# An attention block on one core: where a head's projection products stand among its scores and weighted sums

## The chip, the cores and the metric

The kernel runs on one core of a Trainium2 chip. A core has five engines, each with its own queue of instructions that it works through in order: TensorE (PE, matmuls; its weight loads are listed apart as PEld), VectorE (DVE), ScalarE (ACT), GpSimd (POOL) and SyncE (SP, which only issues transfers here). The metric is the time of one execution on the device in microseconds (us); lower is better.

## The reference

For each of 16 images of 512 channels and 32 x 32 pixels: a group normalisation, q, k and v by one 1x1 convolution, attention with 4 heads of 128 channels over the 1024 pixels, an output projection, and the input added.

```python
xn = ((xg - mu) * jax.lax.rsqrt(var + EPS)).reshape(b, c, h, w)
qkv = jnp.einsum('oc,bchw->bohw', qkv_w, xn) + qkv_b[:, None, None]
...
attn = jax.nn.softmax(jnp.einsum('bhnd,bhmd->bhnm', q, k) * scale, axis=-1)
out = jnp.einsum('bhnm,bhmd->bhnd', attn, v)
...
out = jnp.einsum('oc,bchw->bohw', proj_w, out) + proj_b[:, None, None]
return x + out
```

## The kernel before

Everything is float32. The attention runs over 16 images (b) x 4 heads (h) x 8 key blocks (j) of 128 keys, 512 steps in all. Each step has two halves of 512 queries. A half issues one matmul of scores into a PSUM bank (`s`, line 862), an exponential by ScalarE into `p` (868), and one matmul of the weighted sum of the step before (`po`, 935): the sum lags the scores by one step, so its input has long been there. VectorE adds the finished `p` of a step to a running total (`tot`, 881). A float32 matmul is two passes in the profile, so it appears as two records.

Between these matmuls stand the projections of other data. Each head carries one of them: head 0 the q and k of this image's heads 2 and 3 (`qk_1`), head 1 the output projection of the image before (`pp`), head 2 the q and k of the next image's heads 0 and 1 (`qk_0`), head 3 the next image's v. Each is a matrix product computed by a two-level Strassen scheme. The outer level has seven products, taken in four groups (`OUTER`): three groups of two and, as the last (group 3), a single one. Inside a group the inner level has again seven products, in the order 1, 2, 6, 5, 7, 4, 3 (`strassen`, whose units are the entries of a plan), so that one projection is 28 units. A unit of a group of two is two matmuls of 256 columns (four records), of group 3 one.

Two PSUM banks serve a group. Products 1, 6, 7 and 4 accumulate one after the other in bank `x`: after 1, 6 and 7 ScalarE copies the bank out (`p1`, `u2`, `u3`, line 502), and the next product waits for that copy. Product 2 has a bank `y` of its own; products 5 and 3 share another. VectorE adds a bank and a copy into a result (line 646): c11 from product 2 and `p1`; c22 from product 5's bank and `u3`; c12 from the same bank and `u2`, once product 3 is added to it. So product 3 waits until VectorE has read the bank for c22. c21 is copied by ScalarE (644). For v, VectorE then adds groups (695, 784) and transposes in blocks of 32 (787), and GpSimd sends the result to DRAM (795) and back in another layout (800).

A tile framework orders the instructions of each engine from dependencies, priorities and the order in which the code traces them; it may put a matmul ahead of one traced before it. `tc.issue_after(ins)` makes all instructions of the same engine that its block traces stand behind `ins` in that engine's queue; it adds no wait and doesn't touch other engines.

Before the change `plan_head` spreads the 28 units over 8 key blocks (7 for v) with `spread`. The loop at the end of `fast_path` runs a key block's units after the scores and the weighted sum of each half, the first half of the list behind the first half's sum, the rest behind the second's:

```python
if s > 0:
    weighted_sum(s - 1, half)
n = (len(units) + 1) // 2
run(units[half * n : (half + 1) * n])
```

In the text, "j5.1" is key block 5, second half, and "g3:4" is product 4 of group 3.

Of the kernel before, what the change touches and what calls it, by code (L numbers as in the profile page):

```python
# [186 lines left out]
def fast_path(ctx, tc, x, sources, out, consts, flag, dims):  # L187
# [6 lines left out]
    nc = tc.nc  # L194
    B, C, N, NCC, NH2, NB, GC, SCALE = dims
# [288 lines left out]
    def run(units):  # L484
        for u in units:
            u()
# [322 lines left out]
    def v_block(b, h, j):  # L809
        v, n = vs[b, h // 2], NB // NH2  # L810
        return v[:, h % 2, j, :] if b == 0 else v[:, j // n, h % 2, :, j % n]

    def proj_groups(b):

        ys = {}

        def place(which, r):
            return 2 * (int(which[1]) - 1) + r, int(which[2]) - 1

        def prepare(which, r):  # L820
            o, half = place(which, r)

            own = which == "c12"
            t = ys[which, r] = (tpool if own else ypool).tile(
                [P, HALF], F32, tag=f"ot4{r}" if own else "y", name=f"y_{b}_{o}_{half}"
            )

            eng = nc.sync if own else nc.gpsimd
            dma = eng.dma_start(t, x[b, ts(o, P), ts(half, HALF)])

            tc.add_manual_dep(
                dma.ins, last_eviction[b].ins.name,
                mybir.DependencyInfo(
                    mybir.DependencyClass.Sync, mybir.DependencyReason.DATA
                ),
                reason="residual",
            )

        def finish(which, r, a, c):
            o, half = place(which, r)  # L840
            t = ys.pop((which, r))
            nc.vector.scalar_tensor_tensor(
                t, a, projb_sb[:, o : o + 1], t, ALU.add, ALU.add
            )
            nc.vector.tensor_add(t, t, c)
            nc.gpsimd.dma_start(out[b, ts(o, P), ts(half, HALF)], t)  # L846

        return two_levels(f"pp_{b}", "proj", b, lambda: ob[b], finish, prepare=prepare)
# [4 lines left out]
    steps = B * HEADS * NB  # L853

    def where(s):
        bh, j = divmod(s, NB)
        return (*divmod(bh, HEADS), j)
# [72 lines left out]
    def weighted_sum(s, half):  # L930
        b, h, j = where(s)
        if j == 0:
            po[half] = ps_o.tile([P, HALF], F32, tag=f"o{half}", name=f"po_{b}_{h}_{half}")
        i = ts(half, HALF)
        nc.tensor.matmul(  # L935
            po[half], v_block(b, h, j), ps[s][:, i],
            start=(j == 0), stop=(j == NB - 1),
        )
        if j == NB - 1:
            if (b, h) not in os_:  # L940
                os_[b, h] = opool.tile([P, N], F32, tag="o", name=f"o_{b}_{h}")
            last_eviction[b] = nc.scalar.copy(os_[b, h][:, i], po[half])

    def divide(b, h):
        nc.vector.tensor_mul(os_[b, h], os_[b, h], rinv.pop((b, h)))

    def spread(plan, units, first, last):

        for i, u in enumerate(units):
            plan[first + i * (last - first) // len(units)].append(u)  # L950

    def bias_of_v(o):

        acc = ps_a.tile([P, HALF], F32, tag="y", name=f"pb_{o}")
        half, r = divmod(o, 2)
        for c in range(NCC):
            block = stage["proj"][f"a{half + 1}{c // KC + 1}"]
            nc.tensor.matmul(
                acc[:, 0:1], block[:, ts(r * KC + c % KC, P)], vb_sb[:, c : c + 1],
                start=(c == 0), stop=(c == NCC - 1),  # L960
            )
        nc.vector.tensor_add(
            projb_sb[:, o : o + 1], projb_sb[:, o : o + 1], acc[:, 0:1]
        )

    def kept_group(site, g):
        if g == 0:
            stage_sums(site)
        group_weights(site, g, True)

    def staggered(lists, starts=None):


        starts = starts or (0, 4, 8, 16)[: len(lists)]
        at = [(a + i, g, u) for g, (a, us) in enumerate(zip(starts, lists))
              for i, u in enumerate(us)]
        return [u for _, _, u in sorted(at, key=lambda t: t[:2])]
# [104 lines left out]
    def plan_head(b, h):  # L1082

        plan = [[] for _ in range(NB)]
        if h == 0:
            spread(plan, staggered(next_qk.pop()), 0, NB)
            if b > 0:
                plan[6].append(lambda: o_blocks(b - 1))
                plan[6].append(lambda: sums_of_b(ob[b - 1]))
            else:  # L1090
                plan[5].append(lambda: stage_blocks("v"))
        elif h == 1:
            if b > 0:
                spread(plan, staggered(proj_groups(b - 1)), 0, NB)
            if b + 1 == B:
                plan[0].append(lambda: last_loads("x"))
            else:
                plan[0].append(lambda: load_x(b + 1))
                spread(plan, [lambda c=c: stats_chunk(b + 1, c) for c in range(NCC)], 2, 4)
                gather, scale = stats_group(b + 1)  # L1100
                if b == 0:
                    plan[4] += [gather, scale]
                else:
                    plan[4].insert(0, gather)
                    plan[5].insert(0, scale)
                for r in range(2):
                    plan[5 + r] += [

                        lambda c=c, half=half: normalise(b + 1, c, half, b > 0 or c % 2 == 1)
                        for c in range(KC * r, KC * r + KC) for half in range(NH2)  # L1110
                    ]
                plan[6].append(lambda: x_sums(b + 1, (1,)))
            if b == 0:
                for g in range(len(OUTER)):
                    plan[g // 2].append(lambda g=g: kept_group("v", g))
                    plan[NB // 2 - 1 + g].append(lambda g=g: kept_group("proj", g))
                plan[2].append(lambda: stage_blocks("proj"))
                spread(plan, [lambda o=o: bias_of_v(o) for o in range(NCC)], 3, 5)
        elif b + 1 == B:
            if h == 2:  # L1120
                plan[0].append(lambda: last_loads("w"))
                plan[2].append(last_bias)
            else:
                os_[b, h] = opool.tile([P, N], F32, tag="o", name=f"o_{b}_{h}")
                plan[3].append(lambda: o_blocks(b))
                plan[3].append(lambda: sums_of_b(ob[b], (1,)))
                plan[5].append(lambda: sums_of_b(ob[b], (2, 3), (0,)))
        elif h == 2:
            spread(plan, staggered(qk_groups(b + 1, 0)), 0, NB)

            plan[0].insert(2, lambda: x_sums(b + 1, (2,)))
            plan[1].append(lambda: x_sums(b + 1, (3,)))
        else:

            spread(plan, staggered(next_v.pop()), 0, NB - 1)

            plan[NB - 2].append(lambda: ahead[f"qk_{b + 1}_1"]())
        return plan
# [87 lines left out]
    next_v, next_qk = [], [qk_groups(0, 1)]  # L1226
# [4 lines left out]
    plan = []  # L1231
    for s in range(steps + 1):
        units = []
        if s < steps:
            b, h, j = where(s)
            if j == 0:
                plan = plan_head(b, h)
            units = plan[j]
            if j == NB - 1 and h == 2 and b + 1 < B:
                next_v.append(v_groups(b + 1))  # L1240
                next_qk.append(qk_groups(b + 1, 1))
                units.append(ahead[f"v_{b + 1}"])
        if NB < s < steps and s % NB == 1:
            denominators(*where(s - 2)[:2])
        for half in range(NH2):
            if s < steps:
                scores(s, half)
                if j in (1, 2) and half == 1 and s > NB:
                    with tc.issue_after(exps[s].ins):
                        spread_inverse(*where(s - NB)[:2], j - 1)  # L1250
                if half == 1 and j == 4 and s > NB:

                    with tc.issue_after(added[b, h, 4].ins):
                        divide(*where(s - NB)[:2])
            if s > 0:
                weighted_sum(s - 1, half)
            n = (len(units) + 1) // 2
            run(units[half * n : (half + 1) * n])
        if s < steps and h == 1 and j == 6 and 0 < b < B - 1:
            running_sum(s, 1)  # L1260
        if s > 0:
            del ps[s - 1]
# [136 lines left out]
```

## Time and profile before

| | us |
|---|---|
| three runs | 3161.3, 3164.14, 3161.74 |
| median | 3161.74 |
| profiled execution | 3160.22 |
| its span, first to last instruction | 3158.5 |
| time of one late image (826.64 to 1021.85) | 195.21 |
| VectorE busy in that image | 165.18 |
| ScalarE busy in that image | 90.48 |

How to read the profile's lines: a group's line gives the source line, the engine, the operation, the tiles (output<-inputs), their shapes and the count, then the busy time and the mean duration of one record in ns, then the engine's idle time before them and what ended it. A timeline line gives the start, the time that the merged instructions cover, engine, line, operation, tiles, shapes and count, and in brackets the idle time before and what ended it. Consecutive records of one group are merged (x2, x4). Records of matmuls overlap because matmuls are pipelined, so the time that a matmul costs is read from start to start.

### The profile page before, as it was taken

The numbers are of one execution on the slowest core, as the hardware profiler recorded it, in microseconds if no ns is written. First come the engines' busy times: TensorE is split into PE (matmuls) and PEld (weight loads), VectorE is DVE, ScalarE is ACT, GpSimd is POOL, SyncE is SP. The second block draws the span as 40 slices with busy tenths as digits, with TensorE's granted clock in tenths as the row PEclk, the third lists the DMA queues.
The fourth block names the chain that finished last, engine by engine and source line by source line (L and its number), as shares of the span: only waits on it lengthen the run. The fifth ranks groups of instructions, "written<-read, shape, count | busy, mean of one in ns | idle before, by whom it ended". The sixth has DMA issues, their size and how long they took to land.

```text
span 3158.5 us, 34075 instructions
## 1 busy us (share of the span) xinstructions
PE 3147.1 (100%) x10442; PEld 2181.1 (69%) x10442; DVE 2655.5 (84%) x4687; ACT 1433.7 (45%) x2651; POOL 497.0 (16%) x897
## 2 busy tenths in 40 slices
PE   9999999999999999999999999999999999999999
PEld 7566676676766767677767677677676676767764
DVE  9878979788897888978889787997879978799785
ACT  3535435354353543535435454353534535344433
POOL 0011121111211112111121111212012120121200
PEclk9999999999999999999999999999999999999999
DMA  5555554546545455554555545555455554555531
GB/s 176 187 185 159 184 178 149 177 146 200 167 160 165 150 195 174 167 162 147 193 170 169 169 146 192 168 170 173 142 182 172 174 176 138 179 166 177 188 123 48
DMA packets 210668, 524.83 MB, mean 166 GB/s; under 512 B 32176, under 2 KB 65456, under 8 KB 210480
## 3 DMA queue, kind: packets, MB, share of 16 engines
q1 hardware_dynamic: 133088, 282.39, 28.9%
q0 software_dynamic: 64000, 204.54, 19.2%
q10 hardware_dynamic: 13392, 35.66, 3.5%
q8 instruction: 86, 1.41, 0.2%
q14 instruction: 102, 0.84, 0.1%
HBM read 389.30 MB, written 133.17 MB: 165 GB/s over the span
## 4 chain that ended last, share of the span: by engine, by line
PE 96%; DVE 2%; DMA 1%; issue 0%; SPq 0%; ACT 0%; POOL 0%; ACTq 0%; DVEq 0%; POOLq 0%
PE po L935 27%; PE s L862 27%; PE qk_x L622 12%; PE qk_y L622 9%; PE pp_x L622 6%; PE v_x L622 6%; PE v_y L622 4%; PE pp_y L622 4%; PE lx L1022 0%; DVE qk_t L590 0%; DMA x<-in_x 0%; PE ly L1022 0%; SPq L373 0%; DVE qk L730 0%; DVE qk_r L646 0%
## 5 line engine op out<-in xcount | busy, mean ns | idle before, releaser
L935 PE MATMUL po<-p,v 128*128 128x512 f32 x2048 | 1047.8, 593 | 0.7 <-ACT p L868 0.7
L862 PE MATMUL s<-qk,qk 128*128 128x512 f32 x2048 | 1046.3, 592 | 0.3 <-DVE qk L730 0.3
L868 ACT ACTIVATE p<-s 128x512 f32<-128x512 f32 x1024 | 610.4, 596 | 947.4 <-PE s L862 909.9
L935 PEld LDWEIGHTS po<-p,v 128*128 128x128 f32 x2048 | 604.4, 302 | 320.5 <-issue 213.3
L881 DVE TENSOR_TENSOR tot<-tot,p 128x1024 f32<-128x1024 f32 x385 | 469.5, 1219 | 166.1 <-ACT p L868 166.1
L862 PEld LDWEIGHTS s<-qk,qk 128*128 128x128 f32 x2048 | 388.7, 190 | 89.8 <-issue 29.2
L622 PEld LDWEIGHTS qk_x<-qk_t,w 128*128 128x128 f32 x1344 | 251.7, 190 | 166.7 <-issue 75.3
L622 PE MATMUL qk_x<-qk_t,w 128*128 128x256 f32 x1344 | 356.6, 382 | 0.1
L502 ACT COPY qk_u<-qk_x 128x512 f32<-128x512 f32 (+1 forms) x256 | 136.2, 532 | 230.1 <-PE qk_x L622 230.1
L795 POOL DMA_DIRECT2D vd<-vu x120 | 66.7, 557 | 894.9 <-DVE vu L787 891.7
L646 DVE TENSOR_TENSOR qk_r<-qk_y,qk_u 128x512 f32<-128x512 f32 (+1 forms) x256 | 157.7, 616 | 34.9 <-ACT qk_u L502 21.6
L596 POOL DMA_DIRECT2D kept_t<-qk_t x240 | 129.3, 540 | 274.5 <-DVE qk_t L590 203.9
L646 DVE TENSOR_TENSOR v_r<-v_y,v_u 128x512 f32<-128x512 f32 (+1 forms) x120 | 76.2, 635 | 110.6 <-ACT v_u L502 80.3
L622 PEld LDWEIGHTS pp_x<-pp_t,w_proj 128*128 128x128 f32 x630 | 116.0, 190 | 76.9 <-issue 25.6
L622 PE MATMUL pp_x<-pp_t,w_proj 128*128 128x256 f32 x630 | 168.8, 385 | 0.0
L800 POOL DMA_DIRECT2D v<-vd x240 | 140.6, 592 | 168.1 <-DMA vd<-vu 68.3
L622 PE MATMUL v_x<-v_t,w_v 128*128 128x256 f32 x630 | 166.6, 381 | 0.0
L846 POOL DMA_DIRECT2D out_y<-y x120 | 65.1, 543 | 603.9 <-DVE groups L293 400.6
L622 PEld LDWEIGHTS v_x<-v_t,w_v 128*128 128x128 f32 x630 | 118.4, 190 | 55.3 <-issue 19.1
L622 PE MATMUL qk_y<-x,w 128*128 128x256 f32 x512 | 142.1, 379 | 0.0
L730 DVE SCALAR_TENSOR_TENSOR qk<-qk_r,qkb_sb,qk_r 128x512 f32<-128x512 f32 x192 | 137.6, 743 | 1.6
L502 ACT COPY v_u<-v_x 128x512 f32<-128x512 f32 (+1 forms) x124 | 66.2, 534 | 157.2 <-PE v_x L622 130.4
(214 smaller groups left out, 4449.8 us busy)
## 6 DMA issues: line engine op xcount, KB each, us to landing
w<-kept SPq DMA_DIRECT2D x90, 512.0 KB, 3.9
kept_t<-qk_t POOLq DMA_DIRECT2D x180, 256.0 KB, 3.2
v_t<-kept_t SPq DMA_DIRECT2D x180, 256.0 KB, 2.9
w<-kept SPq DMA_DIRECT2D x90, 384.0 KB, 3.7
rinv<-row ACTq DMA_DIRECT2D x63, 512.0 KB, 4.8
x<-in_x POOLq DMA_DIRECT2D x60, 512.0 KB, 5.0
vd<-vu POOLq DMA_DIRECT2D x120, 256.0 KB, 3.1
v<-vd POOLq DMA_DIRECT2D x240, 128.0 KB, 4.0
```

The costliest lines, as they stand in the source:

```text
L502: nc.scalar.copy(t[n][:, :width], t["x"][:, :width])
L596: nc.gpsimd.dma_start(t, to)
L622: nc.tensor.matmul(acc[:, ts(i, Q)], have["w"][t][:, i, slot, :], inner(i, bn), start=(first and i == 0), stop=True, skip_group_check=True,)
L646: nc.vector.tensor_add(dst, view(a), view(c))
L730: nc.vector.scalar_tensor_tensor(st[b, h][:, ts(half, HALF)], a, qkb_sb[:, i : i + 1], c, ALU.add, ALU.add)
L795: nc.gpsimd.dma_start(rows[which][ts(h, P), :], u)
L800: nc.gpsimd.dma_start(vs[b, pair][ts(q, BLK), half].rearrange("m h (k i) j -> m (h k) (i j)", k=n), rows[which].rearrange("(k m) (q e) -> ...
L846: nc.gpsimd.dma_start(out[b, ts(o, P), ts(half, HALF)], t)
L862: nc.tensor.matmul(sc, ks[b, h][:, ts(j, P)], qs[b, h][:, ts(half, HALF)], start=True, stop=True)
L868: exps[s] = nc.scalar.activation(ps[s][:, ts(half, HALF)], sc, AF.Exp, scale=SCALE)
L881: added[b, h, j] = nc.vector.tensor_add(tot[b, h][:, i], tot[b, h][:, i], ps[s][:, i])
L935: nc.tensor.matmul(po[half], v_block(b, h, j), ps[s][:, i], start=(j == 0), stop=(j == NB - 1),)
```

## The change

The plan of a head keeps empty places where its products stood, and the products go into a list `halfway` by halves: `SIZES` says how many each half takes, 16 halves for a projection laid out over 8 key blocks and 15 for v. In the loop each half takes the next entry of `halfway` and traces it inside `issue_after` of that half's weighted sum, before the half's other units. Other units of the plan run where their index puts them, as before.

```diff
-        nc.tensor.matmul(
+        summed = nc.tensor.matmul(
             po[half], v_block(b, h, j), ps[s][:, i],
             start=(j == 0), stop=(j == NB - 1),
         )
...
+        return summed
...
+    SIZES = {NB: (2, 2, 2, 1, 2, 2, 2, 1, 2, 2, 1, 2, 2, 2, 1, 2),
+             NB - 1: (2, 2, 2, 2, 2, 2, 2, 2, 2, 1, 2, 2, 2, 1, 2)}
+    halfway = []
+
+    def products(plan, units, last):
+        spread(plan, [None] * len(units), 0, last)
+        assert sum(SIZES[last]) == len(units)
+        for n in SIZES[last]:
+            halfway.append(units[:n])
+            units = units[n:]
...
         plan = [[] for _ in range(NB)]
+        halfway.clear()
         if h == 0:
-            spread(plan, staggered(next_qk.pop()), 0, NB)
+            products(plan, staggered(next_qk.pop()), NB)
...
-                spread(plan, staggered(proj_groups(b - 1)), 0, NB)
+                products(plan, staggered(proj_groups(b - 1)), NB)
...
-            spread(plan, staggered(qk_groups(b + 1, 0)), 0, NB)
+            products(plan, staggered(qk_groups(b + 1, 0)), NB)
...
-            spread(plan, staggered(next_v.pop()), 0, NB - 1)
+            products(plan, staggered(next_v.pop()), NB - 1)
...
+            behind = nullcontext()
             if s > 0:
-                weighted_sum(s - 1, half)
+                behind = tc.issue_after(weighted_sum(s - 1, half).ins)
+            if halfway and s < steps:
+                with behind:
+                    run(halfway.pop(0))
             n = (len(units) + 1) // 2
-            run(units[half * n : (half + 1) * n])
+            run(u for u in units[half * n : (half + 1) * n] if u)
```

## The prediction

> **What bounds the kernel now.** I read the page first, then the groups by line with shapes kept apart, then the timeline of one late image (its first scores at 826.64 us, the next image's at 1021.85 us), engine by engine. The page's busy line, clock line and chain of waits:
>
> ```profile
> PE 3147.1 (100%) x10442; PEld 2181.1 (69%) x10442; DVE 2655.5 (84%) x4687; ACT 1433.7 (45%) x2651; POOL 497.0 (16%) x897
> PEclk9999999999999999999999999999999999999999
> PE 96%; DVE 2%; DMA 1%; issue 0%; SPq 0%; ACT 0%; POOL 0%; ACTq 0%; DVEq 0%; POOLq 0%
> ```
>
> TensorE is never shown idle and its clock is full, so no other engine's speed matters by itself. What is left is hidden inside the matmuls' own durations: a matmul held up by its weights is drawn longer, not later. The groups show how much of that there is (count, then busy us and mean ns of one):
>
> ```profile
> L935 PE MATMUL po<-p,v 128*128 128x512 f32 x2048 | 1047.8, 593 | 0.7 <-ACT p L868 0.7
> L862 PE MATMUL s<-qk,qk 128*128 128x512 f32 x2048 | 1046.3, 592 | 0.3 <-DVE qk L730 0.3
> L622 PE MATMUL qk_x<-qk_t,w 128*128 128x256 f32 x1344 | 356.6, 382 | 0.1
> L622 PE MATMUL pp_x<-pp_t,w_proj 128*128 128x256 f32 x630 | 168.8, 385 | 0.0
> L622 PE MATMUL v_x<-v_t,w_v 128*128 128x256 f32 x630 | 166.6, 381 | 0.0
> L622 PE MATMUL v_y<-x,w_v 128*128 128x256 f32 x240 | 67.9, 385 | 0.0
> L622 PE MATMUL v_y<-v_t,w_v 128*128 128x256 f32 x210 | 55.1, 379 | 0.0
> ```
>
> Taking 379 ns as the unhindered 256-column pass, the three x groups carry 3 x 1344 + 6 x 630 + 2 x 630 = 9.1 us too much, v_y 6 x 240 = 1.4 us, and po, against the scores, 1 x 2048 = 2.0 us. So reordering products can win at most about 12.5 us, 0.4% of the span. The end of head 3 in the late image shows all three kinds, on TensorE:
>
> ```profile
> 1006.61 1.02 PE L862 MATMUL s<-qk,qk 128*128 128x512 f32 x2
> 1007.46 1.11 PE L622 MATMUL v_x<-v_t,w_v 128*128 128x256 f32 x4
> 1008.41 1.04 PE L935 MATMUL po<-p,v 128*128 128x512 f32 x2
> 1009.28 1.03 PE L622 MATMUL v_y<-xt,w_v 128*128 128x256 f32 x4
> ...
> 1015.31 0.59 PE L622 MATMUL v_x<-v_t,w_v 128*128 128x256 f32 x2
> 1015.74 1.02 PE L862 MATMUL s<-qk,qk 128*128 128x512 f32 x2
> 1016.60 0.59 PE L622 MATMUL v_x<-v_t,w_v 128*128 128x256 f32 x2
> 1017.03 1.04 PE L935 MATMUL po<-p,v 128*128 128x512 f32 x2
> 1017.90 0.68 PE L622 MATMUL v_y<-x,w_v 128*128 128x256 f32 x2
> 1018.42 1.02 PE L862 MATMUL s<-qk,qk 128*128 128x512 f32 x2
> ...
> 1021.85 1.02 PE L862 MATMUL s<-qk,qk 128*128 128x512 f32 x2
> ```
>
> One score or weighted sum takes 0.86 us from start to start (1018.42 to 1021.85 holds four), a two-part product 0.86, a single one 0.43.
> First kind: the v_x product at 1007.46 (product 4 of group 2) follows product 7 in the same bank with only scores between; it takes 0.95 instead of 0.86. Its weight load waits for the copy out of the bank:
>
> ```profile
> 1006.80 0.58 ACT L502 COPY v_u<-v_x 128x512 f32<-128x512 f32 x1 [1.12 <-PE v_x L622]
> 1007.44 0.73 PEld L622 LDWEIGHTS v_x<-v_t,w_v 128*128 128x128 f32 x4 [0.65 <-ACT v_u L502]
> ```
>
> Second kind: a weighted sum behind a product instead of behind scores (1.04 against 1.02). Its weight load, by the group of the loads, takes 302 ns, and the last pass of a product that could cover it is 0.22 us (half of 0.43):
>
> ```profile
> L935 PEld LDWEIGHTS po<-p,v 128*128 128x128 f32 x2048 | 604.4, 302 | 320.5 <-issue 213.3 <-ACT pp_u L502 3.3 <-ACT p L868 1.5
> ```
>
> Third kind: v_y at 1017.90 (product 3 of group 3) takes 0.68 instead of 0.59. It accumulates into the y bank that VectorE must have read, and VectorE is what to look at:
>
> ```profile
> 998.83 1.23 DVE L881 TENSOR_TENSOR tot<-tot,p 128x1024 f32<-128x1024 f32 x1 [3.62 <-ACT p L868]
> ...
> 1017.07 0.43 DVE L646 TENSOR_TENSOR v_r<-v_y,v_p 128x256 f32<-128x256 f32 x1
> 1017.40 0.43 DVE L646 TENSOR_TENSOR v_r<-v_y,v_u 128x256 f32<-128x256 f32 x1
> 1017.73 1.09 DVE L787 STREAM_TRANSPOSE vu<-vt 128x512 f32<-128x512 f32 x1
> 1018.66 0.68 DVE L784 TENSOR_TENSOR vt<-v_r 128x512 f32<-128x512 f32 x1
> 1019.26 1.21 DVE L881 TENSOR_TENSOR tot<-tot,p 128x1024 f32<-128x1024 f32 x1
> 1020.38 0.42 DVE L646 TENSOR_TENSOR v_r<-v_y,v_u 128x256 f32<-128x256 f32 x1
> ...
> 1023.33 1.15 DVE L787 STREAM_TRANSPOSE vu<-vt 128x512 f32<-128x512 f32 x1 [0.67 <-DMA vd<-vu]
> ```
>
> The add at 1017.40 is c22 (bank y after product 5, plus copy u3); it ends at 1017.83 and product 3 really starts 0.16 later (1017.90 plus the 0.09). The add at 1020.38 is c12, which product 3 makes possible. From 1000.9 to 1022.6 VectorE works off a backlog, as the busy times of that stretch show (its length, then TensorE, weight loads, VectorE, ScalarE, GpSimd): VectorE is busy in 21.67 of 21.70 us.
>
> ```profile
> 1000.90:1022.60 21.70, 21.70 (x68) 14.42 (x67) 21.67 (x32) 7.91 (x15) 4.57 (x8) 1.00 0.52 167
> ```
>
> **The change part by part.** No instruction is added or dropped; only orders change. In the built programs, on TensorE, every product now stands behind its half's weighted sum, and two stretches are shared out anew: the first products of the output projection, and the end of the v projection (numbers are the seven products of a group, PO the weighted sum, g the group):
>
> ```
> head 3   before                 after
> j5.0     s g2:4 PO g2:3 g3:1    s PO g2:4 g2:3
> j5.1     s PO g3:2 g3:6         s PO g3:1 g3:2
> j6.0     s PO g3:5 g3:7         s PO g3:6 g3:5
> j6.1     s g3:4 PO g3:3         s PO g3:7
> j7.0     s PO                   s PO g3:4 g3:3
> j7.1     s PO                   s PO
> ```
>
> On VectorE only this end of v changes, once per image in the 15 images that prepare a next one: c11, c22, transpose, vt, tot, c12 becomes c11, transpose, vt, tot, c22, transpose, vt, qk_t, c12 (and one vu transpose passes the reciprocal). SyncE's queue is the same. On GpSimd the next residual loads pass behind x loads, and a half's v write moves ahead of four v reads; all are used a head later or more. On ScalarE copies and exponentials swap places with a full 0.86 us of weighted sum between.
>
> Removed copy waits (first kind). They stand in one half each of heads 0, 1, 2 and 3, at the start of the projection and near its end:
>
> ```profile
> 1074.04 1.11 PE L622 MATMUL pp_x<-pp_t,w_proj 128*128 128x256 f32 x4
> ...
> 1113.40 0.67 PE L622 MATMUL pp_x<-pp_t,w_proj 128*128 128x256 f32 x2
> ```
>
> Each is 0.08 by length, 0.09 by spacing (0.95 - 0.86): 0.085 us. Behind the weighted sum the copy gets 0.86 us more cover (0.43 in the last of these places), so all go: six an image. One of the six, in head 1, gains nothing, because its product 3 already starts on VectorE's heels:
>
> ```profile
> 1107.82 0.68 DVE L646 TENSOR_TENSOR pp_r<-pp_y,pp_u 128x512 f32<-128x512 f32 x1
> 1108.66 1.03 PE L622 MATMUL pp_y<-ot,w_proj 128*128 128x256 f32 x4
> ```
>
> c22 there ends at 1108.50, and 0.16 later is the start that it has. So 5 x 15 x 0.085 = 6.4 us; the sixth would be 1.3 to 1.5 more if VectorE's add came sooner.
> Removed waits of weighted sums (second kind): about 11 places an image; 2.0 us by the group over 165 of them is 0.012 each; without the head 1 place 10 x 15 x 0.012 = 1.8 us.
> The third kind goes as such, 15 x 0.09 = 1.4 us, but something takes its place. Saved in all: 9.6 us.
>
> [...]
>
> Added: the wait of product 3 of v's last group. TensorE from 1006.61, at 0.86 (0.43) a product: 3.44 for j5.0, 2.58, 2.58, 2.15 and then s, PO, product 4 (2.15) brings product 3 up at 1019.51. VectorE reaches the same c22 later: it takes the place of the old one, behind transpose (1018.66 - 1017.73 = 0.93), vt (0.60) and tot (1.12). 1017.40 + 2.65 = 1020.05, end 1020.48; plus 0.16, product 3 starts at 1020.64. The wait is 1.13 us. Queued behind it on TensorE are the scores and sums of j7.1 and the whole next head; nothing covers it. The VectorE times are the old ones, since in that stretch it has 0.03 us of idle time in which TensorE could have moved it. Bounds: no less than 0.97 (add's end, no latency); no more than 1.46, if c22 only starts where c12 did (1020.38). I take 1.13, by its own rows: 15 x 1.13 = 16.95 us (14.6 to 21.9). c12 then is queued later than product 3's end and waits for nothing.
>
> Sum: -6.4 - 1.8 - 1.4 + 16.95 = +7.3 us. The profiled execution took 3160.2 us around its span of 3158.5, so 3167.5 in its terms; the median of the runs is 1.5 higher at 3161.7, so 3169.0. Bounds: 14.6 - 9.6 - 1.5 = +3.5 and 21.9 - 9.6 = +12.3, that is 3165 to 3174.
>
> **The rivals.** (a) Faster: VectorE gets c22 done before 1019.35. Place: the backlog of head 3; price then 0, so -9.6, 3152 us. It holds in full from 1.13 us less backlog; the balance tips to faster below a wait of 9.6 / 15 = 0.64 us. For it: VectorE's last idle time, 3.62 us before 998.83, is close by. Against: every row after it is back to back, and the built order puts the three long instructions ahead. (b) Half of it: a wait near 0.6 us, -9.6 + 9 = 3161 us. For it: hundredths in each VectorE step; against it: they would have to add up to 0.5 us, and the same rows repeat in every image. (c) The weight loads find no new cover, so that only the third kind goes: -1.4 + 16.95, 3177 us. For it the 0.085 us themselves, which are uncovered load; against it the two busy shares above. [...] (d) A second wait: v's later half comes too late for key block 4 of the next image.
>
> ```profile
> 1036.94 2.34 POOL L800 DMA_DIRECT2D v<-vd  x4 [0.72 <-DMA vd<-vu]
> ...
> 1055.42 1.02 PE L935 MATMUL po<-p,v 128*128 128x512 f32 x2
> ```
>
> The reads are issued by 1039.3, block 4 is used at 1055.4: 16 us in hand, to be lost before the first us counts; if two were lost, 15 x 2 more, 3199 us. That the products don't move at all is excluded by the built order.
>
> **How the numbers follow.** Forecast 0.78, (a) 0.11, (b) 0.07, (c) 0.02, (d) 0.02. 0.2% is 6.3 us, about what a measurement of this kernel can tell from no change; the forecast's 3.5 to 12.3 lies on both sides of it, about 0.59 beyond and 0.19 within. Slower 0.59 + 0.04 = 0.63, same 0.19 + 0.07 = 0.26, faster 0.11. The range, 3158 to 3174, holds the forecast and (b) and leaves out (a), (c) and (d); the forecast's own is 3165 to 3174.
>
> **What would show it.** In the changed profile: x groups at 379 to 380 ns and po at 592 (first two kinds); one v_y product an image that starts its second pass about 1.1 us late, shown as length (the mean of v_y<-x rises from 385 to 379 + 16950 / 240 = 450 ns) or as idle time before it; its weight load released by the VectorE add; image spacing 195.21 + 0.5 us. Less than 0.64 us there means that the backlog was shorter, and the sum's sign is wrong; x groups still above 381 mean that the weighted sum doesn't cover the copies.

## The result, and the profile after

The changed kernel takes 3169.74 us (median of 15 runs, 3168.08 to 3172.49) against 3162.61 us before (15 runs, 3160.74 to 3164.24): 7.1 us slower, ratio 1.0023, 95% interval 1.0015 to 1.0031. The profiled execution has a span of 3167.1 us.

The page's busy line and chain of waits of the changed kernel:

```profile
PE 3142.6 (99%) x10442; PEld 2199.9 (69%) x10442; DVE 2659.1 (84%) x4687; ACT 1446.1 (46%) x2651; POOL 497.8 (16%) x897
PE 90%; DVE 8%; DMA 1%; issue 1%; ACT 0%; SPq 0%; POOL 0%; ACTq 0%; DVEq 0%; POOLq 0%
```

VectorE, 2% of the chain before, now has 8%: the chain goes back from each new wait into VectorE's backlog. The groups of TensorE with shapes kept apart:

```profile
L862 PE MATMUL s<-qk,qk 128*128 128x512 f32 x2048 | 1047.0, 593 | 0.3 <-DVE qk L730 0.3
L935 PE MATMUL po<-p,v 128*128 128x512 f32 x2048 | 1046.4, 593 | 0.7 <-ACT p L868 0.7
L622 PE MATMUL qk_x<-qk_t,w 128*128 128x256 f32 x1344 | 353.9, 380 | 0.1
L622 PE MATMUL pp_x<-pp_t,w_proj 128*128 128x256 f32 x630 | 165.4, 379 | 0.0
L622 PE MATMUL v_x<-v_t,w_v 128*128 128x256 f32 x630 | 165.3, 379 | 0.0
L622 PE MATMUL v_y<-x,w_v 128*128 128x256 f32 x240 | 68.0, 386 | 13.3 <-DVE v_r L646 13.3
```

The x groups fell from 382, 385 and 381 ns to 380, 379 and 379: the copy waits are gone. The weighted sums no longer take longer than the scores (1046.4 us busy against 1047.0). Against that stands an idle time that the kernel before did not have, 13.3 us ahead of v_y, released by VectorE's add. One late image takes 195.74 us (829.42 to 1025.16), 0.53 more than before; the prediction named 0.5. One image's end of head 3, TensorE and then VectorE:

```profile
1019.73 1.02 PE L862 MATMUL s<-qk,qk 128*128 128x512 f32 x2
1020.59 1.02 PE L935 MATMUL po<-p,v 128*128 128x512 f32 x2
1021.45 0.59 PE L622 MATMUL v_x<-v_t,w_v 128*128 128x256 f32 x2
1022.91 0.70 PE L622 MATMUL v_y<-x,w_v 128*128 128x256 f32 x2 [0.87 <-DVE v_r L646]
1023.45 1.02 PE L862 MATMUL s<-qk,qk 128*128 128x512 f32 x2
```

```profile
1019.42 0.44 DVE L646 TENSOR_TENSOR v_r<-v_y,v_p 128x256 f32<-128x256 f32 x1
1019.75 1.13 DVE L787 STREAM_TRANSPOSE vu<-vt 128x512 f32<-128x512 f32 x1
1020.68 0.72 DVE L784 TENSOR_TENSOR vt<-v_r 128x512 f32<-128x512 f32 x1
1021.28 1.24 DVE L881 TENSOR_TENSOR tot<-tot,p 128x1024 f32<-128x1024 f32 x1
1022.40 0.45 DVE L646 TENSOR_TENSOR v_r<-v_y,v_u 128x256 f32<-128x256 f32 x1
```

Product 4 starts at 1021.45, so product 3 could start 0.43 later, at 1021.88. It is drawn at 1022.91 and 0.11 us longer than its 0.59: 1.14 us lost. The bracket says less, 0.87, because the matmul before it is drawn 0.16 past the time at which the next could start. VectorE shows why: c22 stands at 1022.40, 2.98 us behind c11, with transpose, vt and tot between.

### The profile page after: what moved, and what is told of

The parts are those of the page before. It is cut to its first block, busy times and chain, and to the rows that moved or that the text cites. A ratio compares the mean times of both kernels' runs of the same rounds, so it can differ in the third digit from the quotient of the medians.

```text
span 3167.1 us, 34165 instructions
## 1 busy us (share of the span) xinstructions
PE 3142.6 (99%) x10442; PEld 2199.9 (69%) x10442; DVE 2659.1 (84%) x4687; ACT 1446.1 (46%) x2651; POOL 497.8 (16%) x897
## 4 chain that ended last, share of the span: by engine, by line
PE 90%; DVE 8%; DMA 1%; issue 1%; ACT 0%; SPq 0%; POOL 0%; ACTq 0%; DVEq 0%; POOLq 0%
PE s L862 26%; PE po L935 25%; PE qk_x L622 12%; PE qk_y L622 9%; PE pp_x L622 6%; PE v_x L622 4%; PE pp_y L622 4%; PE v_y L622 4%; DVE tot L881 1%; DVE vu L787 1%; DVE v_r L646 1%; DVE qk_t L590 1%; DVE vt L784 1%; DVE v_r L695 1%; DVE o L946 1%
## 5 line engine op out<-in xcount | busy, mean ns | idle before, releaser
L862 PE MATMUL s<-qk,qk 128*128 128x512 f32 x2048 | 1047.0, 593 | 0.3 <-DVE qk L730 0.3
L935 PE MATMUL po<-p,v 128*128 128x512 f32 x2048 | 1046.4, 593 | 0.7 <-ACT p L868 0.7
L935 PEld LDWEIGHTS po<-p,v 128*128 128x128 f32 x2048 | 616.4, 301 | 376.8 <-issue 256.0
L644 ACT COPY qk_r<-qk_x 128x512 f32<-128x512 f32 (+1 forms) x128 | 68.3, 533 | 147.7 <-PE qk_x L622 112.5
```

What stands on the lines that cost most here:

```text
L644: nc.scalar.copy(dst, view(a))
L862: nc.tensor.matmul(sc, ks[b, h][:, ts(j, P)], qs[b, h][:, ts(half, HALF)], start=True, stop=True)
L935: summed = nc.tensor.matmul(po[half], v_block(b, h, j), ps[s][:, i], start=(j == 0), stop=(j == NB - 1),)
```

## The experiments

All ratios are to the kernel before, measured beside each run (median 3160.82 us for experiments 1 to 4, 3160.80 for 5 to 8).

**1. Product 3 later, c22 in its old place.** The last group of v keeps products 4 and 3 in j7.0, but products 1, 6 and 7 each come a half earlier, and j6.1 stays empty. The code traces c22 together with product 7, so it comes earlier too.

```diff
-             NB - 1: (2, 2, 2, 2, 2, 2, 2, 2, 2, 1, 2, 2, 2, 1, 2)}
+             NB - 1: (2, 2, 2, 2, 2, 2, 2, 2, 2, 1, 3, 2, 2, 0, 2)}
```

> As the changed kernel, but v's last group is laid out so that product 7 stands in the second half... of no importance by itself: g2:4, g2:3, g3:1 in j5.0, g3:2 and 6 in j5.1, g3:5 and 7 in j6.0, nothing in j6.1, g3:4 and 3 in j7.0 as in the changed kernel. On VectorE c22 is then again the instruction right behind c11. Theory (product 3 waits for c22, which stands behind three VectorE instructions): no wait in j7.0, all savings of 9.6 us stay, 3162.6 - 9.6 = 3153.0 us, ratio to before 0.9970; v_y products at 379 ns and no idle time before them. Rival (products of v in key block 7, or behind the sums, cost by themselves): about as the changed kernel, 3170 us.

Measured: 3151.74 us against 3160.82, ratio 0.9971 (0.9960 to 0.9982). The order on VectorE, and then product 3 on TensorE:

```profile
1014.99 0.45 DVE L646 TENSOR_TENSOR v_r<-v_y,v_p 128x256 f32<-128x256 f32 x1
1015.32 0.45 DVE L646 TENSOR_TENSOR v_r<-v_y,v_u 128x256 f32<-128x256 f32 x1
```

```profile
1017.03 0.59 PE L622 MATMUL v_x<-v_t,w_v 128*128 128x256 f32 x2
1017.47 0.59 PE L622 MATMUL v_y<-x,w_v 128*128 128x256 f32 x2
1017.90 1.02 PE L862 MATMUL s<-qk,qk 128*128 128x512 f32 x2
```

c22 directly follows c11 and is done 1.7 us before product 3, which starts 0.44 after product 4 like any product. So neither key block 7 nor a place behind the sums costs anything; the layout turns from 7.1 us slower to 9.1 us faster when c22 is not held back and product 3 comes well behind it. This run moves products on TensorE as well; the next one moves none.

**2. One VectorE instruction moved.** TensorE's order is that of the changed kernel; in v's last group the pending additions and transposes are held until c22 is traced and then queued behind it. Of the three instructions ahead of c22 that moves only vt; behind c22 the qk_t addition passes a transpose and a vt.

```diff
-                        nc.vector.tensor_add(dst, view(a), view(c))
+                        first[g, which] = nc.vector.tensor_add(dst, view(a), view(c))
...
-                    with placed():
+                    held = site == "v" and g == len(OUTER) - 1
+                    if held and (g, "c11") in first and (g, "c22") not in first:
+                        return
+                    with (
+                        tc.issue_after(first[g, "c22"].ins)
+                        if held and (g, "c22") in first else placed()
+                    ):
...
-        pending = []
+        pending, first = [], {}
```

> TensorE's order as in the changed kernel; on VectorE only the vt addition (0.60 us) is held behind c22, transpose and running total stay ahead of it. Theory: c22 starts at 1017.40 + 0.93 + 1.12 = 1019.45 on the clock of the profile of before, ends 0.43 later, product 3 0.16 after that at 1020.04 instead of 1020.64, so the wait is 0.53 instead of 1.14 us: 15 x 0.61 = 9.1 us under the changed kernel's 3169.7, 3160.6 us, ratio to before 0.9994. Rival (the wait has nothing to do with VectorE's order): 3169.7.

Measured: 3159.82 us, ratio 0.9998 (0.9989 to 1.0007). TensorE and VectorE:

```profile
1018.59 0.59 PE L622 MATMUL v_x<-v_t,w_v 128*128 128x256 f32 x2
1019.45 0.70 PE L622 MATMUL v_y<-x,w_v 128*128 128x256 f32 x2 [0.26 <-DVE v_r L646]
```

```profile
1016.54 0.46 DVE L646 TENSOR_TENSOR v_r<-v_y,v_p 128x256 f32<-128x256 f32 x1
1016.88 1.13 DVE L793 STREAM_TRANSPOSE vu<-vt 128x512 f32<-128x512 f32 x1
1017.83 1.24 DVE L887 TENSOR_TENSOR tot<-tot,p 128x1024 f32<-128x1024 f32 x1
1018.96 0.43 DVE L646 TENSOR_TENSOR v_r<-v_y,v_u 128x256 f32<-128x256 f32 x1
```

Product 3 could start at 1019.02 and really starts at 1019.45 + 0.11: 0.54 us, where 0.53 was expected. With 1.14 in the changed kernel and none in experiment 1 that makes three points, and the time follows them: 15 waits of 0.54 are 8.1 us, about what the rest saves. The intervals of this run and of the changed kernel don't overlap, and in the two traces TensorE, ScalarE and GpSimd run the same instructions in the same order, so the order on VectorE is shown to be the cause.

**3 and 4. The change in parts: heads 0 to 2 alone, head 3 alone.** The one keeps `spread` for v, the other keeps it for the three other projections.

```diff
 (experiment 3)
-            products(plan, staggered(next_v.pop()), NB - 1)
+            spread(plan, staggered(next_v.pop()), 0, NB - 1)
 (experiment 4)
-            products(plan, staggered(next_qk.pop()), NB)
+            spread(plan, staggered(next_qk.pop()), 0, NB)
...
-                products(plan, staggered(proj_groups(b - 1)), NB)
+                spread(plan, staggered(proj_groups(b - 1)), 0, NB)
...
-            products(plan, staggered(qk_groups(b + 1, 0)), NB)
+            spread(plan, staggered(qk_groups(b + 1, 0)), 0, NB)
```

> The change in heads 0, 1 and 2 alone; v in head 3 as in the kernel before. Theory: the savings without head 3's, 9.6 - 1.3 - 0.2 - 1.4 = 6.7 us, so 3155.9 us, ratio 0.9979, and no new wait over 0.2 us an image. Rival (the loss is spread over all heads: products behind sums are slower everywhere): 3163 us or more.

> The change in head 3 alone; heads 0, 1 and 2 as in the kernel before. Theory: 15 x 1.14 = 17.1 us of new wait less 2.9 us of head 3's own savings: +14.2 us, 3176.8 us, ratio 1.0045. With the run of heads 0 to 2 it adds up to the change. Rival (the loss is spread over all heads): +5 us or less, 3167.

Measured: heads 0 to 2 alone 3153.77 us, ratio 0.9978 (0.9968 to 0.9988); head 3 alone 3175.74, ratio 1.0044 (1.0031 to 1.0058). That is -7.1 and +14.9 us, in sum +7.9, beside +7.1 for the whole. The groups in the two runs, heads 0 to 2 first:

```profile
L622 PE MATMUL pp_x<-pp_t,w_proj 128*128 128x256 f32 x630 | 165.4, 379 | 0.0
L622 PE MATMUL v_x<-v_t,w_v 128*128 128x256 f32 x630 | 166.7, 381 | 0.0
L622 PE MATMUL v_y<-x,w_v 128*128 128x256 f32 x240 | 68.0, 385 | 0.0
```

```profile
L622 PE MATMUL pp_x<-pp_t,w_proj 128*128 128x256 f32 x630 | 168.8, 385 | 0.0
L622 PE MATMUL v_x<-v_t,w_v 128*128 128x256 f32 x630 | 165.3, 379 | 0.0
L622 PE MATMUL v_y<-x,w_v 128*128 128x256 f32 x240 | 68.1, 386 | 13.3 <-DVE v_r L646 13.3
```

Each part carries its own rows and leaves the other's as they were: the projection's x at 379 with v as before, and the other way round. The loss is all in head 3.

**5 and 6. The two halves of the idea: queueing and layout.** Experiment 5 keeps `issue_after` and gives `SIZES` the halves of the old layout; experiment 6 keeps the layout and drops `issue_after`.

```diff
 (experiment 5)
-    SIZES = {NB: (2, 2, 2, 1, 2, 2, 2, 1, 2, 2, 1, 2, 2, 2, 1, 2),
-             NB - 1: (2, 2, 2, 2, 2, 2, 2, 2, 2, 1, 2, 2, 2, 1, 2)}
+    SIZES = {NB: (2, 2, 2, 1, 2, 2, 2, 1, 2, 2, 2, 1, 2, 2, 2, 1),
+             NB - 1: (2,) * 14}
 (experiment 6)
-                behind = tc.issue_after(weighted_sum(s - 1, half).ins)
+                weighted_sum(s - 1, half)
```

> Products behind their half's weighted sum, but in the halves of the old layout (two products of a bank may share a half, and then the second still goes to the next half, ahead of its sum). In the built order the places j5.1 and j7.1 of heads 0 to 2 and j5.0 of head 3 stay as before; j6.1 of head 0, j0.0, j3.1 and j6.1 of head 1 and j6.1 of head 3 are mended. Theory: 0.2 + 1.2 + 0.2 + 1.2 = 2.8 us saved, nothing in head 3, where VectorE sets product 3: 3160.8 - 2.8 = 3158.0 us, ratio 0.9991. Rival (the queueing is what saves, the layout only adds the wait): ratio 0.9979 or less.

> The layout over halves without the queueing behind the sums. The built order is that of the changed kernel on all engines. Theory (layout alone orders the products): as the changed kernel, ratio 1.0023. Rival (the queueing does something that the order does not show): a ratio outside 1.0015 to 1.0031.

Measured: queueing alone 3158.56 us against 3160.80, ratio 0.9991 (0.9982 to 1.0000): 2.2 us less where 2.8 was expected, in an interval that reaches to no change. Its profile shows where it saves: the projection's x group falls from 168.8 us busy to 166.6, while those of q and k (356.5) and of v (166.6) stay as before. Layout alone: 3168.91, ratio 1.0027 (1.0016 to 1.0038), as the changed kernel; TensorE and VectorE run in the changed kernel's order. So the layout makes that order, gain and loss, without the queueing. What the queueing adds is seen only with the old layout, where two products of a bank can share a half.

**7. v's end in the halves of before, behind the sums.**

```diff
-             NB - 1: (2, 2, 2, 2, 2, 2, 2, 2, 2, 1, 2, 2, 2, 1, 2)}
+             NB - 1: (2, 2, 2, 2, 2, 2, 2, 2, 2, 1, 3, 2, 2, 2)}
```

> The changed kernel, with v's end in the halves of before (g3:4 and g3:3 in j6.1) but behind the sums. c22 stands right behind c11 as before. Theory: product 3 of v's last group starts when VectorE's c22 is done, as before, so that head 3 saves nothing: in j6.1 a wait of 0.19 us (before 0.095 plus 0.015 there and 0.098 in j5.0), and the whole 6.7 us under the run before. Rival (a product behind its sum has no wait): j6.1 without a wait and 9.6 us saved.

Measured: one run, 3155.09 us, 5.7 us under the median of the runs before (3160.80). One run can't tell 6.7 from 9.6; the timeline can. TensorE in j6.1, then VectorE's c22:

```profile
1016.66 0.59 PE L622 MATMUL v_x<-v_t,w_v 128*128 128x256 f32 x2
1017.20 0.70 PE L622 MATMUL v_y<-x,w_v 128*128 128x256 f32 x2
1017.73 1.02 PE L862 MATMUL s<-qk,qk 128*128 128x512 f32 x2
```

```profile
1016.67 0.47 DVE L646 TENSOR_TENSOR v_r<-v_y,v_u 128x256 f32<-128x256 f32 x1
```

From product 4 to the next scores it takes 1.07 instead of 0.86: 0.21 us of wait, 0.19 expected. What TensorE saved ahead of it, it waits here, since VectorE's c22 sets the start of product 3: it ends at 1017.14, and product 3 really starts at 1017.20 + 0.11, 0.17 later. Here, taking out the wait in front of a dependency that was just met only moved the wait.

**8. The sixth place.** Experiment 1's kernel, with the division on VectorE that stands in head 1 (for the head before) moved from key block 4 to 5.

```diff
-                if half == 1 and j == 4 and s > NB:
+                if half == 1 and j == (5 if h == 1 else 4) and s > NB:
...
-                    with tc.issue_after(added[b, h, 4].ins):
+                    with tc.issue_after(added[b, h, j].ins):
```

> The kernel with the gap in v, and in head 1 the division of the head before on VectorE (1.2 us) moved from key block 4 to key block 5, so that c22 of the output projection's group 2 is no longer behind it. Theory: the wait of 0.12 us in j5.1 of head 1, which is the sixth place that gained nothing, goes: 14 x 0.12 = 1.7 us under the kernel with the gap, 3150.1 us, ratio 0.9966, and the trace has no wait there. Rival (that place is set by something else, ScalarE's copy): the wait stays, 0.9971.

Measured: 3150.54 us, ratio 0.9968 (0.9956 to 0.9980), 1.2 us under experiment 1; the intervals overlap, so the times alone don't tell them apart. Products 4 and 3 of group 2 in j5.1 of head 1, in experiment 1 and then here:

```profile
1105.23 1.03 PE L622 MATMUL pp_x<-pp_t,w_proj 128*128 128x256 f32 x4
1106.11 1.13 PE L622 MATMUL pp_y<-ot,w_proj 128*128 128x256 f32 x4
```

```profile
1104.20 1.03 PE L622 MATMUL pp_x<-pp_t,w_proj 128*128 128x256 f32 x4
1105.06 1.03 PE L622 MATMUL pp_y<-ot,w_proj 128*128 128x256 f32 x4
```

The 0.12 us (0.88 for 0.86, and 1.13 for 1.03) are gone, so VectorE's queue was what held this place. This version has the lowest median of the study, 10.3 us under the kernel before.

## Why the prediction was right

- Copy waits, -6.4 us for five places: all five are gone, as the x groups at 379 to 380 ns show. By busy time the three x groups lost 7.4 us and pp_y<-ot, where the sixth place's wait now is, gained 1.4 (48.7 to 50.1): 6.0 net. The run of heads 0 to 2, which holds four of them and most of the po waits, has -7.1 us where 6.7 was expected.
- The sixth place, 0 us: it was named as set by VectorE, and in the changed profile its wait stands in front of product 3 instead of product 4. It costs slightly more there than in the kernel before: the rows of experiment 1, shown under experiment 8, give 0.12 us, while 0.10 (0.085 and 0.012) was saved. Experiment 8 shows the cause.
- Waits of the weighted sums, -1.8 us: po and s have the same mean after (593 ns).
- The new wait, 15 x 1.13 = 16.95 us: 1.14 us in the image shown. The three VectorE steps, 2.65 us on the rows of before, came out as 2.65 (1019.75 to 1022.40). The choice of 1.13, by the old rows, held between its bounds of 0.97 and 1.46; the backlog was not shorter, and the time scaled with it in experiments 1 and 2.
- The sum, +7.3 us, 3169.0: measured +7.1, 3169.74. It lay close to the bound of 0.2% (6.3 us) as was said; the interval reaches to both sides of it. Agreement within 0.2 us is partly luck: the interval runs from 4.7 to 9.8 us, and a stretch at half the clock, described below, can move an execution by 1.7. What the runs do support is the size of the terms: 1.14 us an image for the wait, and -7.1 and +14.9 us for the two parts.
- Rival (a), VectorE early enough, is refuted by the wait's 1.14 us; what it would have given, 9.6 us, is experiment 1's -9.1. Rival (b), a wait near 0.6 us, is refuted by the same 1.14; experiment 2, which takes one of the three steps away, has such a wait (0.54). Rival (c), no new cover for the weight loads, fails on the x groups (382, 385 and 381 ns before, 380, 379 and 379 after) and on experiment 3 (-7.1 us). The two busy shares against it are those of weight loads and matmuls in the page's busy line: 69% and 100% of the span before, 69% and 99% after, so most of the loads' time passes while matmuls run. Rival (d) left no row: no weighted sum waits for the reads of v (the one idle time listed ahead of a sum after the change is 0.7 us, ended by ScalarE's `p`, as before).
- One marker was told loosely: the wait would be drawn as a longer v_y mean or as idle time. It is mostly idle time, 13.3 us of some 17, and the rest is length and the drawn end of the matmul before.
- The place behind the weighted sum, on which the savings rest, comes from the layout and not from the queueing (experiments 5 and 6). No term of the sum hung on which of the two it was.

## What to carry to other kernels

TensorE, busy throughout here (100% of the span before), has small waits (0.08 to 0.11 us) drawn inside its instructions, and a group's mean against that of an unhindered group finds them (381 to 385 ns against 379). The reordering on TensorE also reordered VectorE, which feeds it: with three instructions between c11 and c22 the wait was 1.14 us, with two 0.54, and with none and product 3 coming later (experiment 1) nothing. So look for the place where a helper engine works off a backlog, and see what now stands ahead of the one instruction that the busy engine needs. Between the changed kernel (+7.1 us) and experiment 1 (-9.1) lie 16 us. Most of it goes with c22's place right behind c11 (experiment 7, one run: -5.7), and the rest, about 3 us, with the empty half between the product that makes c22's input ready and the one that needs its result. So the better layout here is the one that leaves VectorE the time, not the one that packs TensorE's halves evenly.

## What was unexpected in the hardware

In six of the ten profiled executions (the changed kernel and experiments 3 to 7) the mean granted clock of TensorE is 0.999, in the other four 1.000. In the changed kernel's, TensorE runs for 3.4 us of the first image at half its clock; in that of before it doesn't. The same stretch in the changed kernel's profile and then in that of before (length, then the engines, the granted clock as the last figure but two):

```profile
130.80:134.20 3.40, 3.40 (x6) 1.32 (x5) 2.97 (x12) 2.02 (x5) 0.00 (x0) 0.50 0.29 117
```

```profile
130.80:134.20 3.40, 3.40 (x10) 1.49 (x9) 2.97 (x13) 2.50 (x6) 0.00 (x0) 1.00 0.31 126
```

In the changed kernel it follows a stretch in which TensorE has only one-column matmuls and a wait:

```profile
126.94 0.28 PE L959 MATMUL pb<-vb_sb,st_a 128*128 128x1 f32 x2
127.84 2.10 PE L959 MATMUL pb<-vb_sb,st_a 128*128 128x1 f32 x14 [0.63 <-DMA st_a<-in_proj_wT]
129.81 1.11 PE L862 MATMUL s<-qk,qk 128*128 128x512 f32 x2
130.75 1.88 PE L935 MATMUL po<-p,v 128*128 128x512 f32 x2
132.43 1.90 PE L862 MATMUL s<-qk,qk 128*128 128x512 f32 x2
134.13 1.05 PE L935 MATMUL po<-p,v 128*128 128x512 f32 x2
```

The sum at 130.75 and the scores at 132.43 take 1.68 and 1.70 us from start to start instead of 0.86. So half the clock for 3.4 us costs 1.7 us, and it is in the difference of the two profiled spans (8.6 us) but not in the prediction's sum, which gives 7.3. The runs of the changed kernel fit it: ten with a mean granted clock of 0.999 take 3170.2 us on average, five with 1.000 take 3168.5. In the run of experiment 6 a stretch elsewhere in the first image has the same 0.50:

```profile
159.30:162.60 3.30, 3.30 (x10) 2.55 (x9) 1.52 (x2) 1.17 (x2) 0.46 (x1) 0.50 0.61 227
```

What decides which executions are hit is not shown. The one-column matmuls alone don't: the kernel before has the same sixteen records of them, from 127.24 to 129.75 with a wait of 0.27 us, and its clock behind them is 1.00.
